# Routing beside attention in layer 0, and another order of work in layer 1, in a four-layer attention and expert stack

## The chip, the cores and the metric

The kernel runs on one core of one Trainium2 chip. The metric is the device time of one execution in microseconds (us). The core's engines are TensorE (PE; its weight loads are listed as PEld), VectorE (DVE), ScalarE (ACT), GpSimd (POOL) and SyncE (SP, which issues most transfers). Each has its own queue, taken in order, and they wait for each other through semaphores.

## The reference

`x` is 4 batches of 512 tokens of width 128, `ctx` 4 batches of 154 tokens. Eight residual steps follow each other: four layers, each an attention from x to ctx and then a mixture of 8 experts. What matters here:

```python
def _L0_xattn_ref(encoder_hc, decoder_hq, w_sim, b_sim, W_qv, b_qv):
    Sim = (encoder_hc @ w1)[:, :, None] + (decoder_hq @ w2)[:, None, :] + \
          jnp.einsum('bid,bjd->bij', encoder_hc * w3, decoder_hq) + b_sim[0]
    A = softmax(Sim, axis=2)
    hq_hat = jnp.einsum('bij,bjd->bid', A, decoder_hq)
    Batt = softmax(jnp.max(Sim, axis=2), axis=1)
    hc_bar = jnp.einsum('bi,bid->bd', Batt, encoder_hc)[:, None, :]
    hc_hat = jnp.broadcast_to(hc_bar, encoder_hc.shape)
    feats = concatenate([encoder_hc, hq_hat, encoder_hc * hq_hat, encoder_hc * hc_hat], axis=-1)
    return feats @ W_qv + b_qv

x = x + _L0_xattn_ref(_layernorm(x), ctx, ...)
x = x + _L0_ffn_ref(_layernorm(x), ...)           # top 2 of 8 experts, silu gate
x = x + _L1_xattn_ref(ctx, ctx, _layernorm(x), mask, ...)   # 16 heads of 8
x = x + _L1_ffn_ref(_layernorm(x), ...)           # top 1 of 8 experts, with a capacity
x = x + _L2_xattn_ref(...)                        # 16 heads of 64
...
```

Layer 1's attention is a masked softmax over the 154 context tokens for each of 16 heads of width 8, then the product with V and a projection by `Wo`.

## The kernel before, in words

Tokens are handled in tiles of 128: a batch has `NI` = 4 of them. Experts work on two halves, each of two batches. For a half, `route` computes norms, logits, the top experts, the rank of each token within its expert and from these a slot for each token (`su`) and a list of the expert of each block (`eb`). It is a generator: each `yield` is a point at which its caller can put other work, and `Steps.step(n)` advances it by n such steps. The normalised tokens are then written to their slots in DRAM by indirect transfers on POOL (`scatter`, L721). These row transfers are first put into a list, `rows_due`; `row_transfers(n, behind)` starts up to n of them, and with `behind` each of them waits for that instruction, so that they are paced by the work beside them. `experts` loads blocks of tokens (`tok`, L838, which waits for all row transfers of the half), transposes them (L848), multiplies them by the weights of their expert (`up`, L875; `down`, L906) and stores the results; `gather` puts indirect loads of the results (L939) into `rows_due`, and `combine` adds them to x (L957).

Layer 0's attention (`layer0_setup`) works on a whole batch at a time: `prepare(b)` normalises and transposes x, computes `Sim` as two products, one with the scaled context (L979) and one with the row term `w2b` (L980), copies it to SBUF with the scalar `bsim` added (L983, into `sim`, of which there is one buffer), and takes its maxima and exponentials. `tile_of` normalises the probabilities (L1004), transposes them (L1008, L1013), multiplies by the context, computes the batch-wide softmax (L1034 and L1036 are its weighted sum and its sum of weights), builds the last three of the four features (L1042 to L1044) and multiplies the four by W_qv (L1049). `attend_first` runs the four batches; the first half's routing is begun after batch 2's turn, and its row transfers come after all four batches. In this part the order of instructions on each engine is chosen by a planner, which takes the order of the program as priority and its own estimates of durations.

Layer 1's attention works tile by tile, in 16 periods, in an order written out by hand on PE, ACT and DVE (`attend_all`, `narrow_period`). A period holds the scores and exponentials of tile `new` beside the products with V of tile `old`. Scores come in three groups of heads: `score(g)` on PE (L1141 mask, L1150), `most(g)` on DVE (L291, the negated maximum), `exp(g)` on ACT (L305). `score(0)` and `most(0)` of the next tile, `nxt`, come at the end of a period. For `old`: `turn_ends` and `turn(n)` transpose the probabilities on PE, `take_ends` and `take(n)` copy them on DVE (L261), `by_v_ends` and `by_v(n)` are the products with V (L381, L405), and `scaled` multiplies by the inverse sums (L412). The inverse sums are spread over the partitions by `replicate`: a transposition (L332), a copy (`rT`, L334), a store to DRAM (L339) and a load (L340, `rep`). `project` (L422) and `residual` end a tile. `parts` prepares the next batch, one part in each of four periods: mask, norm and values, the transposed norm, keys and queries. `middle` and `after` take one step of the work beside: combining the experts' results of layer 0, then routing for layer 1.

PSUM holds two buffers of each of three kinds, given out in turn: `sc` for scores, `tr` for transposes and small products, `av` for products with V. A new use waits for the readers of the use before the last.

Of the kernel before, what the change touches and what calls it, by code (L numbers as in the profile page):

```python
# [19 lines left out]
P = 128  # L20
# [6 lines left out]
E = 8  # L27
# [19 lines left out]
def tile_xattn_moe_stack(ctx: ExitStack, tc: tile.TileContext, a: dict, out: bass.AP):  # L47
# [33 lines left out]
    turn = [0]  # L81

    def evac(o, i, scale=None):

        turn[0] += 1
        if turn[0] % 2:
            if scale is None:
                nc.vector.tensor_copy(o, i)
            else:
                nc.vector.tensor_scalar(o, i, scale, None, ALU.mult)  # L90
        elif scale is None:
            nc.scalar.copy(o, i)
        else:
            nc.scalar.activation(o, i, AF.Copy, scale=scale)
# [10 lines left out]
    x = []  # L105
    for b in range(B):
        t = xpool.tile([P, NI, D], F32, tag=f"x{b}", name=f"x{b}")
        nc.sync.dma_start(t, x_in[b])
        x.append(t)
# [3 lines left out]
    nc.sync.dma_start(ctail, a["ctx_1024"][:, P:S2, :].rearrange("b k d -> k b d"))  # L113

# [89 lines left out]
    def columns(src, rows, name):  # L204

        t = p2.tile([rows, P], F32, tag="rows", name=f"{name}_r")
        nc.sync.dma_start(t, src)
# [224 lines left out]
    def narrow_period(new, old, nxt=None, middle=nothing, queries=nothing, parts=nothing, after=nothing):  # L432
# [9 lines left out]
        if old:  # L442
            old.turn_ends()
            old.turn(0)
        if new:
            new.most(1)
            new.exp(0)
            new.exp(1)
        if old:
            old.take_ends("v")  # L450
            old.take(0, "v")
            old.by_v_ends()
            old.turn(1)
            old.take(1, "v")
        if new:
            new.score(2)
        if old:
            old.turn(2)
            old.by_v(0)
            old.by_v(1)  # L460
        if new:
            new.most(2)
            new.exp(2)
        if old:
            old.take(2, "v")
            old.turn(3)
            old.by_v(2)
            old.take(3, "v")
# [3 lines left out]
        parts()  # L472
        if nxt:
            nxt.score(0)
            nxt.most(0)
# [4 lines left out]
        if new:  # L480
            new.replicate()
        if old:
            old.project()
            old.residual()
        after()

    def wide_period(new, old, nxt=None, middle=nothing, queries=nothing, parts=nothing, after=nothing):
# [472 lines left out]
    def layer0_setup():  # L960
        wsim = columns(a["L0_xattn_w_sim"].rearrange("(k p) -> k p", p=P), 3, "wsim")
# [437 lines left out]
```

## Time and profile before

| | us |
|---|---|
| median of 3 runs | 1300.3 |
| lowest and highest | 1290.47, 1302.03 |
| profiled execution, its own time | 1392.88 |
| span of its instructions | 1390.8 |
| mean granted TensorE clock in it | 0.902 |

The profiled execution takes longer than the timed runs, so stages and sums are read in its own time and related to the median afterwards. In the groups of the page a line of a helper stands for all its callers: L261 is every copy by `copy` on DVE, L305 every exponential of layers 1 to 3. "[... <- X]" after a line of the timeline is the idle time of that engine before it and what ended it. "x2" counts instructions; an fp32 product is two of them.

### The profile page before, as it was taken

The page shows a single profiled execution, that of the slowest core. Times are in us where ns is not written, and L with a number is a line of the kernel's source. Part 1 is how long each engine was busy: PE and PEld are TensorE (multiplying, and loading weights), DVE is VectorE, ACT ScalarE, POOL GpSimd, SP SyncE. Part 2 cuts the span into 40 slices and gives each one's busy share as a digit, 9 for nine tenths or more (in the row PEclk, how much of TensorE's full clock was granted, in tenths as well). Part 3 has the DMA queues.
Part 4 walks back from the last instruction along what each step waited for, and adds up shares of the span by engine and source line. Part 5 has one row for each costly group of instructions (what it writes and reads, how often), then busy time and mean ns, then how long its engine had stood idle before and what let it go on. Part 6 is the DMA issues. An engine that isn't in the chain of part 4 may idle for free.

```text
span 1390.8 us, 26946 instructions
## 1 busy us (share of the span) xinstructions
PE 1125.7 (81%) x9435; PEld 924.2 (66%) x9435; DVE 736.2 (53%) x2057; ACT 575.6 (41%) x2290; POOL 252.9 (18%) x281
## 2 busy tenths in 40 slices
PE   5876998976777689788999988657879999898881
PEld 3766997833344348776878767646668778787771
DVE  4563546546667655235667665314456667454442
ACT  1113333543454444355665554212545655432220
POOL 2031314031000101302000031332220000304224
PEclk8787999968998879999999999767999999899996
DMA  6014685611010215532212224442321112245652
GB/s 210 1 65 118 207 251 182 196 51 29 9 22 27 70 27 141 148 98 47 47 32 56 54 66 121 120 124 80 116 47 39 40 33 47 66 109 142 179 163 69
DMA packets 136995, 126.80 MB, mean 91 GB/s; under 512 B 13466, under 2 KB 116511, under 8 KB 136479
## 3 DMA queue, kind: packets, MB, share of 16 engines
q1 hardware_dynamic: 129695, 110.39, 28.6%
q0 software_dynamic: 7168, 14.69, 3.7%
q8 instruction: 77, 1.26, 0.4%
q14 instruction: 55, 0.45, 0.1%
HBM read 101.31 MB, written 23.72 MB: 90 GB/s over the span
## 4 chain that ended last, share of the span: by engine, by line
PE 36%; DVE 8%; issue 4%; ACT 4%; DMA 4%; another core or an unknown queue 3%; POOL 1%; SPq 1%; POOLq 0%; DVEq 0%; ACTq 0%
PE sc L875 5%; PE sc L608 5%; PE av L405 4%; PE av L906 4%; PE tr L368 4%; PE tr L422 4%; DMA w<-in_up 3%; ACT probs L305 2%; PE sc L593 2%; PE av L387 2%; DVE nm L291 2%; PE sc L557 1%; POOL yg L939 1%; DVE aT L412 1%
## 5 line engine op out<-in xcount | busy, mean ns | idle before, releaser
L305 ACT ACTIVATE probs<-sc,nm 128x154 f32<-128x154 f32 x768 | 287.0, 402 | 193.6 <-DVE nm L291 178.4
L875 PE MATMUL sc<-tokT,w 128*128 128x128 f32 x1528 | 214.6, 290 | 19.8 <-DMA w<-in_up 14.8
L875 PEld LDWEIGHTS sc<-tokT,w 128*128 128x128 f32 x1528 | 195.0, 202 | 31.0 <-DMA w<-in_up 11.1
L906 PE MATMUL av<-w,hT 128*128 x1160 | 179.2, 292 | 42.7 <-issue 19.2
L291 DVE TENSOR_REDUCE nm<-sc 128x6 f32<-128x924 f32 x144 | 143.2, 1010 | 100.7 <-PE sc L608 47.9
L906 PEld LDWEIGHTS av<-w,hT 128*128 128x128 f32 x1160 | 155.9, 201 | 53.9 <-issue 22.9
L305 ACT ACTIVATION_READ_ACCUMULATOR probs<-sc,nm 128x1 f32 x768 | 168.0, 219 | 0.0
L939 POOL DMA_INDIRECT yg<-ybuf,su x112 | 107.0, 956 | 295.5 <-DVE ys L914 67.1
L233 POOL TENSOR_TENSOR rstd<-ve,nhalf 128x4 f32<-128x4 f32 x32 | 33.1, 1034 | 652.4 <-DVE ve L231 544.4
L721 POOL DMA_INDIRECT buf<-xn,su x112 | 108.4, 968 | 184.0 <-DVE eb L744 78.7
L261 DVE COPY pT<-tr 128x512 f32<-128x512 f32 x160 | 107.3, 687 | 62.0 <-PE tr L368 48.6
L368 PE MATMUL tr<-ident,probs 128*128 128x128 f32 x768 | 123.9, 293 | 0.7 <-DVE rT L334 0.7
L405 PE MATMUL av<-pT,vm 128*64 128x128 f32 (+1 forms) x1536 | 104.5, 285 | 18.4 <-DVE pT L261 16.8
L368 PEld LDWEIGHTS tr<-ident,probs 128*128 128x128 f32 x768 | 88.0, 148 | 29.4 <-issue 14.5
L914 DVE COPY ys<-av 128x128 f32<-128x128 f32 x168 | 48.0, 286 | 111.2 <-PE av L906 73.4
L405 PEld LDWEIGHTS av<-pT,vm 128*64 128x64 f32 (+1 forms) x1536 | 65.2, 127 | 46.8 <-DVE pT L261 25.9
L891 ACT ACTIVATE eg<-sc,w 128x128 f32<-128x128 f32 x184 | 52.9, 370 | 89.2 <-PE sc L875 52.2
L608 PE MATMUL sc<-kT,qT 64*128 64x154 f32 x1024 | 85.1, 304 | 3.5 <-ACT probs L305 3.5
L895 DVE SCALAR_TENSOR_TENSOR hT<-sc,w,eg 128x128 f32<-128x128 f32 x184 | 55.9, 342 | 53.4 <-ACT eg L891 50.6
L608 PEld LDWEIGHTS sc<-kT,qT 64*128 64x128 f32 x1024 | 69.8, 186 | 14.5 <-issue 10.1
L593 PE MATMUL sc<-xnT,wq 128*128 128x128 f32 x512 | 70.8, 296 | 2.9 <-ACT probs L305 2.9
L593 PEld LDWEIGHTS sc<-xnT,wq 128*128 128x128 f32 x512 | 64.9, 206 | 8.2 <-issue 4.3
(252 smaller groups left out, 1504.8 us busy)
## 6 DMA issues: line engine op xcount, KB each, us to landing
w<-in_up SPq DMA_DIRECT2D x46, 516.0 KB
w<-in_up SPq DMA_DIRECT2D x76, 258.0 KB
rep<-rd SPq DMA_DIRECT2D x64, 256.0 KB
ybuf<-ys SPq DMA_DIRECT2D x168, 64.0 KB
tok<-buf SPq DMA_DIRECT2D x36, 256.0 KB
w<-in_down SPq DMA_DIRECT2D x3, 2048.0 KB
w<-in_up SPq DMA_DIRECT2D x46, 128.0 KB
buf<-zero SPq DMA_DIRECT2D x2, 1472.0 KB
```

What stands on the lines that cost most here:

```text
L261: return nc.vector.tensor_copy(o, i)
L291: nc.vector.tensor_reduce(self.at.heads(self.nm, g, n), self.sc[g][:, :, 0 : n * S2].rearrange("p j (s k) -> p j s k", s=n), AX.X, ALU.max ...
L305: nc.scalar.activation(self.pr[:, h, :], self.sc[g][:, j, s * S2 : (s + 1) * S2], AF.Exp, bias=self.nm[:, h : h + 1], accum_out=self.rs[:, ...
L368: nc.tensor.transpose(q[:, t * P : (t + 1) * P], self.pr[:, h, 0:P], ident)
L405: nc.tensor.matmul(av[rows, cols], v, self.pT[n][:, t, :], start=False, stop=last)
L593: nc.tensor.matmul(sc[:, c // 4, c % 4 * P : (c % 4 + 1) * P], wq[:, c * P : (c + 1) * P], at.xnT[:, i * P : (i + 1) * P], start=True, sto ...
L608: nc.tensor.matmul(sc[:, j, s * S2 : (s + 1) * S2], at.qT[i][rows, c, :], at.kT[rows, c, :], start=True, stop=True)
L721: ins = nc.gpsimd.indirect_dma_start(out=buf[half], out_offset=bass.IndirectOffsetOnAxis(ap=su[:, t : t + 1], axis=0), in_=xns[t // NI][:, ...
L875: nc.tensor.matmul(dst, w[:, at : at + P], xT, start=True, stop=True)
L895: products.append(nc.vector.scalar_tensor_tensor(hT[:, fc, :], up, b0, g, ALU.add, ALU.mult))
L906: nc.tensor.matmul(y[:, 0:D], hT[:, fc, :], w2[:, bass.ds(e, 1), fc, :].rearrange("p o d -> p (o d)"), start=(fc == 0), stop=(fc == nf - 1),)
L939: ins = nc.gpsimd.indirect_dma_start(out=yg[:, t, :], out_offset=None, in_=ybuf[half], in_offset=bass.IndirectOffsetOnAxis(ap=su[:, t : t ...
```

## The change

In layer 0:
- `Sim`'s row term is computed once for all batches, with `bsim`, into `row`; `prepare` does one product a tile and adds `row` while copying. `sim` has two buffers.
- the product of x with the broadcast average is folded into the weights: `wc` is the first block of W_qv plus the fourth scaled by the average, and three products remain of four. The sum of weights is taken by the exponential's accumulator and one product.
- `attend_first` prepares a batch or two ahead, and begins routing after batch 1; row transfers go two at a time behind four instructions each of batches 2 and 3.
- the rows and the context are loaded ahead of the other inputs; the experts' gates are loaded after layer 0's own weights.

In layer 1:
- `nxt.score(0)` and `nxt.most(0)` come between `by_v(1)` and `turn(3)`; `parts` comes after `take(1)`; `middle` after the next maximum.
- `replicate` of `old` comes at the start of its period, after `score(1)`; `project` and `residual` come one period later (`older`).
- keys and queries use a `tr` and an `av` buffer instead of an `sc` buffer.
- `evac`, which alternates between DVE and ACT, uses DVE alone during this attention (`busy`).

`ordered_all` holds the same three engines that `ordered` held.

```diff
-        if turn[0] % 2:
+        if turn[0] % 2 or busy[0]:
...
-    def narrow_period(new, old, nxt=None, middle=nothing, queries=nothing, parts=nothing, after=nothing):
+    def narrow_period(new, old, nxt=None, middle=nothing, queries=nothing, parts=nothing, after=nothing, older=None):
...
         if new:
             new.score(1)
-        if old:
-            old.turn_ends()
-            old.turn(0)
-        if new:
             new.most(1)
             new.exp(0)
-            new.exp(1)
+        if older:
+            older.project()
+            older.residual()
         if old:
+            old.replicate()
+            old.turn_ends()
             old.take_ends("v")
+            old.turn(0)
             old.take(0, "v")
             old.by_v_ends()
             old.turn(1)
             old.take(1, "v")
+        parts()
         if new:
+            new.exp(1)
             new.score(2)
-        if old:
-            old.turn(2)
-            old.by_v(0)
-            old.by_v(1)
-        if new:
             new.most(2)
             new.exp(2)
         if old:
+            old.by_v(0)
+            old.turn(2)
             old.take(2, "v")
+            old.by_v(1)
+        if nxt:
+            nxt.score(0)
+            nxt.most(0)
+        if old:
             old.turn(3)
+            old.take(3, "v")
             old.by_v(2)
-            old.take(3, "v")
             old.by_v(3)
             old.scaled(0)
         middle()
-        parts()
-        if nxt:
-            nxt.score(0)
-            nxt.most(0)
         if new:
             new.short()
             new.inverse()
         queries()
-        if new:
-            new.replicate()
-        if old:
-            old.project()
-            old.residual()
         after()
...
+        row = w1.tile([P, B, S2], F32, tag="wv", name="row")
+        sc = ps_sc()
+        for j in range(2):
+            nc.tensor.matmul(
+                sc[:, j, 0 : 2 * S2],
+                w2b,
+                ctxT[:, 2 * j : 2 * j + 2, :].rearrange("p b k -> p (b k)"),
...
-                nc.tensor.matmul(dst, xnT[:, i * P : (i + 1) * P], rhs1[:, b, :], start=True, stop=False)
-                nc.tensor.matmul(dst, w2b, ctxT[:, b, :], start=False, stop=True)
-            sim = p2.tile([P, NI, S2], F32, tag="aT", name="sim", bufs=1)
+                nc.tensor.matmul(dst, xnT[:, i * P : (i + 1) * P], rhs1[:, b, :], start=True, stop=True)
+            sim = p2.tile([P, NI, S2], F32, tag="probs", name="sim")
...
-            evac(pm, q)
+            row_transfers(2, evac(pm, q))
...
-            evac(pt, q[0:ST, :])
+            row_transfers(2, evac(pt, q[0:ST, :]))
...
-            nc.scalar.activation(ebt, md, AF.Exp)
+            es = small.tile([P, 1], F32, tag="es", name="es")
+            nc.scalar.activation(ebt, md, AF.Exp, accum_out=es)
...
-            for i in range(NI):
-                nc.tensor.matmul(hcp[:, 1:2], ones, ebt[:, i : i + 1], start=(i == 0), stop=(i == NI - 1))
+            nc.tensor.matmul(hcp[:, 1:2], ones, es, start=True, stop=True)
...
+            wc = p2.tile([P, D], F32, tag="res1", name="wc")
+            nc.vector.scalar_tensor_tensor(wc, wqv[:, 3, :], hc, wqv[:, 0, :], ALU.mult, ALU.add)
+            ft = p2.tile([P, 2, S], F32, tag="vm", name="ft")
+            row_transfers(2, nc.scalar.copy(ft[:, 0, :], hq))
...
-                sc = ps_sc()
-                nc.tensor.matmul(sc[:, 0, 0:S2], bd["Wk"], ctxT[:, b, :], start=True, stop=True)
-                nc.tensor.matmul(sc[:, 1, :], bd["Wq"], at.xnT, start=True, stop=True)
+                k, q = ps_tr(), ps_av()
+                nc.tensor.matmul(k[:, 0:S2], bd["Wk"], ctxT[:, b, :], start=True, stop=True)
+                nc.tensor.matmul(q, bd["Wq"], at.xnT, start=True, stop=True)
...
-        beside = Steps(idle())
-        tiles = prepare(0, found[0])
-        for b in range(B):
-            tiles(0)
-            if b == 1:
-                found.update({k: stats(x[k]) for k in range(2, B)})
-            if b == 2:
-                beside = Steps(route(layer, 0, *gates[layer]))
-            if b < B - 1:
-                tiles = prepare(b + 1, found[b + 1])
-            if b == 2:
-                beside.step(6)
+        tiles = [prepare(b, found[b]) for b in range(2)]
+        tiles[0](0)
+        tiles.append(prepare(2, found[2]))
+        tiles[1](0)
+        beside = Steps(route(layer, 0, *gates[layer])).step(3)
+        tiles.append(prepare(3, found[3]))
+        beside.step(5)
+        tiles[2](0)
+        beside.step(1)
+        tiles[3](0)
         return beside.finish()
...
-        if last:
-            (narrow_period if layer == 1 else wide_period)(None, last)
+        if layer == 1:
+            narrow_period(None, last, older=late)
+            last.project()
+            last.residual()
+        elif last:
+            wide_period(None, last)
```

## The prediction

> **What bounds the kernel now.** I read the page first, then windows of busy time by stage, then the timeline where a window showed idle engines.
>
> ```profile
> span 1390.8 us, 26946 instructions
> PE 1125.7 (81%) x9435; PEld 924.2 (66%) x9435; DVE 736.2 (53%) x2057; ACT 575.6 (41%) x2290; POOL 252.9 (18%) x281
> PE   5876998976777689788999988657879999898881
> PEclk8787999968998879999999999767999999899996
> ```
>
> TensorE is the busiest engine, but over the span that average mixes stages. The change touches two: layer 0's attention (slices 1 to 4) and layer 1's attention (slices 8 to 15, where PE falls to 6 and 7 and the granted clock sags). The windows of layer 0, cut where each batch's scores are copied out and where the first expert product starts:
>
> ```profile
> core 0: us, PE busy (x) PEld busy (x) DVE busy (x) ACT busy (x) POOL busy (x), PEclk, DMA share, GB/s
> 36.66:53.88 17.22, 14.84 (x85) 12.53 (x84) 10.60 (x35) 3.10 (x11) 1.01 (x1) 0.80 0.00 1
> 53.88:70.85 16.97, 15.28 (x89) 12.97 (x88) 10.54 (x35) 3.70 (x12) 1.01 (x1) 0.80 0.00 1
> 70.85:93.91 23.06, 21.64 (x157) 19.37 (x156) 17.19 (x73) 4.34 (x14) 3.17 (x3) 0.85 0.04 9
> 93.91:117.59 23.68, 3.62 (x21) 2.74 (x20) 5.50 (x24) 0.00 (x0) 14.47 (x15) 0.58 0.37 128
> ```
>
> A batch takes 17 us, 85% of it PE work; then come 23.7 us in which PE works 3.6. The timeline says what fills them:
>
> ```profile
> 90.87 0.16 DVE L744 TENSOR_SCALAR eb<-ef 1x23 int32<-1x23 f32 x1
> 91.18 1.19 POOL L721 DMA_INDIRECT buf<-xn,su  x1 [8.46 <-DVE eb L744]
> ...
> 110.38 0.96 POOL L721 DMA_INDIRECT buf<-xn,su  x1 [0.30 <-issue]
> 112.77 5.28 SPq L838 DMA_DIRECT2D tok<-buf  x4
> 115.72 1.94 PE L848 MATMUL tr<-ident,tok 128*128 128x128 f32 x8 [15.59 <-DMA tok<-buf]
> 117.59 5.70 PE L875 MATMUL sc<-tokT,w 128*128 128x128 f32 x32
> ```
>
> The routing table is ready at 90.9; 16 row transfers of 1.26 us each follow one another on POOL until 111.3 (20.2 us); only then can the token load start, and PE waits for it.
>
> Layer 1 has 16 periods, cut here at the first maximum of each tile:
>
> ```profile
> 281.00:301.61 20.61, 13.24 (x83) 6.50 (x83) 8.78 (x18) 6.81 (x33) 7.65 (x8) 0.67 0.12 32
> 367.33:379.38 12.05, 9.35 (x85) 5.05 (x85) 8.15 (x16) 6.81 (x33) 0.00 (x0) 1.00 0.06 12
> 379.38:394.01 14.63, 10.15 (x85) 5.22 (x85) 8.91 (x15) 7.29 (x34) 0.00 (x0) 1.00 0.05 10
> 407.42:422.09 14.67, 9.40 (x85) 5.10 (x85) 11.65 (x37) 6.81 (x33) 2.02 (x2) 0.99 0.15 46
> ```
>
> No engine is full in any of them. A period is a chain of PE and DVE waiting for each other, 12 us at the least and 15.5 on average (272.35 to 520). The longest hold indirect transfers:
>
> ```profile
> 285.51 0.32 SPq L340 DMA_DIRECT2D rep<-rd  x1
> 299.58 0.29 DVE L412 TENSOR_TENSOR aT<-av,rep 128x128 f32<-128x128 f32 x1 [5.02 <-PE sc L1150]
> 371.75 0.32 SPq L340 DMA_DIRECT2D rep<-rd  x1
> 377.45 0.29 DVE L412 TENSOR_TENSOR aT<-av,rep 128x128 f32<-128x128 f32 x1 [0.55 <-PE av L405]
> ```
>
> The scaling that needs the replicated sums waited until 14 us after their load was issued in a period with eight row gathers; in a quiet one it was free 5.7 us after the issue.
>
> **What the skill says.** *DMA: Bandwidth & Descriptors*, section *Anatomy of one DMA*, gives a fixed cost of about 2 us a transfer; here L340, which waits for L339's data, follows it by 2.4 us (369.36 to 371.75), which agrees. *TensorE: Matmul & The Clock Gate*, section *Why this matters for your kernels*, says to leave no PE gap over some 3 us between bursts, or the clock falls to half; the trace agrees: 0.67 around the stalls of 281 to 301, 1.00 in 367 to 394. *DMA*, section *Queues, rings and completion order*: each DMA engine goes round its queue rows packet by packet; whether gathers hold up the load of the sums in this way, no run here shows.
>
> **The change, layer 0.** (a) PE work. The row product (L980) leaves every batch: 8 instructions at 0.13 us (0.26 at half clock), 1.0 to 2.1 us. The products with W_qv go from 32 to 24 at 0.11 to 0.21: 0.9 to 1.7. The sums with ones (L1036) go from 8 to 2 at 0.12: 0.7. Together 2.6 to 4.5, middle 3.4 at this clock; for four batches 13.6 less, and 4 instructions of twice the width come back once (1 to 2). (b) DVE: the 0.55 us product L1044 goes, a 128x128 one (0.35, L957's form) and a column one (0.15) come. The score copy takes a tensor operand instead of a scalar: L983 takes 0.53, the SBUF-only L1004 takes 0.80 for twice the width, so -0.1 to +0.1 each: nothing. ACT gains one 0.19 us accumulator read. (c) The routing starts after batch 1 instead of beside batch 3. PE work from 19.1 to 93.9 was 63.6 us of 74.8 (the windows shown and 11.8 in 19.1 to 36.7); it falls to 52. At the same busy share attention would end at 80 instead of 93.9; but its order is the planner's, and the routing's small DVE steps now stand among the copies, so I take half: 87. (d) The table: batch 1 was done at 64.9 and should be at about 56; from there the table took 26 us amid other work, and its own steps sum to some 14 (statistics and norm 4.5, transposes to logits 3.8, two maxima 2.4, ranks and slots 3), so it is ready between 70 and 82; the transfers then need 20.2, to 90 to 102. (e) Pacing holds the last pair behind the last batch's output copy, at about 86, to 89. POOL's other work is the 1 us powers of the norms: those of batches 2 and 3 stand behind the paced transfers, as they stood behind all 16 before (111.37). I take 93 for the last transfer against 111.3: **-18 us**, bounds -9 to -23. Loading rows and context ahead of the other inputs shortens the front by 1 to 2 us, which the wider row product takes back. What follows has PE busy 32 to 34 us of each 35 from 140 to 280, so the shift is kept.
>
> **Layer 1.** Take the plain order at full clock with the durations of 367 to 379: a score group 1.5 (the short one 1.1), four transposes 0.58, a copy 0.60 (0.69 to its end), a maximum 1.04, a product group 0.36, DVE to PE 0.2. Before: 12.05, or 11.5 without the 0.5 of xnT. After, from the start of score 1 at 0: score 1 to 1.5; projection and replication on PE to 2.0; maximum 1 to 2.6, residual's first step to 2.95. The projection and the end transposes use the same of two buffers, so these *now wait for the residual*: 3.15 to 3.75, turn 0 to 4.3, copies to 5.0, turn 1 to 5.55, score 2 to 6.65, by_v 0, turn 2, by_v 1 to 7.9, next score 0 to 9.4, turn 3 to 9.95, next maximum on DVE to 10.5, copy 3 to 11.1, last product 11.3 to 11.7. That is 11.7: the next scores do not wait any more, but 1.2 us are lost at the front and 1.0 before the last product. Plain periods: 0. Gains come where something stood between the last product and the next scores: three periods with values (norm, two products: DVE 2.0) and three with keys and queries (PE 1.5, DVE 1.43, ACT 0.6, in series). These now stand mid-period, yet cost PE and DVE time there, and the query copy delays exp 1: about 1 us each, 6 in all. Routing and combining steps (DVE 1.3 to 2.7) come after the next maximum: 0.4 in eight periods, 3. Against it: the mask of batches 2 and 3 shares buffers with the value ends, so its load starts after by_v_ends (344.65 before); now its use follows 1.2 us later instead of 4.7. Landing takes 2 to 4.7, so the DVE queue, with copies and maximum 2 behind it, waits 1 to 3.5 us twice; I take 1.5 each. Sum -6; the copies that DVE takes over from ACT lie in its slack of a third of a period. Last tile: one projection and one residual move into layer 1's experts, under 1 us. **-6 us**, bounds -20 (the stalls beside transfers shrink too) to +10 (lower clock by the new front wait).
>
> **Sum.** 1392.9 (the profiled execution; its span is 1390.8) - 24 = 1369. The median run is 1300.3, or 0.9335 of that; with it the saving is 22 us: **1278**. From here 1% is what a measurement can tell from no change: 1287.3 and 1313.3.
>
> **Rivals.** *Layer 0 gains, layer 1 loses what it gains* (front wait and mask wait weigh more; for: the hand count gives nothing in plain periods): -18 + 4 = -14, 1287. *Layer 1's transfer stalls go as well* (the first maximum now precedes them; for: some 20 us of periods 20.6, 19.1 and 23.7 are stall; against: no reason of theirs is removed): -24 - 15, 1264. *The routing isn't moved in effect*: the planner keeps the table behind attention, the 20 us stay, and only fewer products count: -10 in all, 1291. *Slower: the sums arrive late.* From the copy of the sums to the scaling it was 8.1 us in a quiet period (369.3 to 377.45); now it is 3.4 to 11.7, 8.3. If the load takes longer than 8.3, each period grows by the rest; if it takes the 12 to 14 us seen beside gathers everywhere, 15 periods grow by about 3.7: +55 - 18 = +37, 1335. It decides from about 11 us on. Against: the quiet periods bound it to 8.1.
>
> **How the numbers follow.** Forecast 0.44; layer 1 nothing 0.20; stalls go 0.14; routing not moved 0.11; sums late 0.11. The second is split at its edge (1287). Faster by over 1%: 0.44 + 0.14 + 0.10 = 0.68; within 1%: 0.10 + 0.11 = 0.21; slower 0.11. The range goes down past the rival at 1264 with the full -23 in layer 0, to 1258, and up to 1302, past the unmoved routing with layer 1 at +10.
>
> **What would show it.** Right: last row transfer of layer 0 near 93 and first expert product near 99; PE busy in that gap; layer 1 about 6 us shorter with a 1 us wait of the end transposes for the residual. Wrong: a table after 85, transfers still in a bare row, scalings that wait for a DMA in quiet periods, or a mean clock in layer 1 under 0.8.

## The result and the profile after

| | us |
|---|---|
| before, median of 20 runs | 1298.6 |
| after, median of 20 runs | 1291.2 (1281.5 to 1299.0) |
| ratio after / before | 0.9944, 95% interval 0.9924 to 0.9963 |
| forecast | 1278 (1258 to 1302) |

By the ratio the change saves 7.3 us, 0.56% (by its interval 4.8 to 9.9 us). The direction was as forecast, the size a third of the 22 us.

First the base. The profile that the forecast was worked on has a span of 1390.8 us; the kernel before, profiled again as `e0`, has one of 1299.7. One row of the groups, first from the forecast's profile and then from the new one (after the bars: busy time and mean of one, then the idle time ahead of the group and what ended it), shows what the first had besides:

```profile
L914 DVE COPY ys<-av 128x128 f32<-128x128 f32 x168 | 48.0, 286 | 111.2 <-PE av L906 73.4 <-remote 29.7 <-DMA w<-in_up 3.5
```

```profile
L914 DVE COPY ys<-av 128x128 f32<-128x128 f32 x168 | 48.2, 287 | 75.0 <-PE av L906 69.4 <-DMA ybuf<-ys 5.3
```

Same copies, same duration, but 29.7 us of idle time whose releaser the profile does not know ("remote"). Such stalls, up to 8.9 us long, stand in several groups of the forecast's profile; neither `e0` nor the profile after shows one. So the profiles below are read against `e0`. The page after, the span and three rows:

```profile
span 1289.8 us, 26803 instructions
PE 1094.4 (85%) x9351; PEld 897.6 (70%) x9351; DVE 739.7 (57%) x2066; ACT 572.4 (44%) x2290; POOL 252.4 (20%) x281
PE   4787998987877789889999989957899999899881
PEclk8668999998998789999999999879999999999996
```

The second and third digits of the clock row already show the surprise of layer 0: 6 and 6, where `e0` has 7 and 8 and an attention with less work was expected to be denser. Its windows, cut at the forecast's times (busy time and count of PE, PEld, DVE, ACT, POOL, then clock and DMA):

```profile
core 0: us, PE busy (x) PEld busy (x) DVE busy (x) ACT busy (x) POOL busy (x), PEclk, DMA share, GB/s
36.70:54.00 17.30, 14.30 (x75) 12.34 (x75) 10.26 (x36) 3.27 (x13) 1.01 (x1) 0.70 0.00 1
54.00:71.00 17.00, 8.55 (x37) 7.86 (x36) 10.11 (x42) 2.53 (x10) 1.01 (x1) 0.60 0.00 0
71.00:94.00 23.00, 21.28 (x108) 14.67 (x109) 13.22 (x57) 3.49 (x9) 13.69 (x14) 0.72 0.34 112
```

From 54 to 71, where the routing now stands, PE works 8.6 of 17 us instead of 15.3. The timeline of the way to the first expert product:

```profile
74.84 0.16 DVE L742 TENSOR_SCALAR eb<-ef 1x23 int32<-1x23 f32 x1
75.15 1.19 POOL L719 DMA_INDIRECT buf<-xn,su  x1 [16.29 <-DVE eb L742]
...
91.84 0.96 POOL L719 DMA_INDIRECT buf<-xn,su  x1 [0.30 <-issue]
...
99.12 0.69 DVE L1067 TENSOR_TENSOR x<-x,res 128x512 f32<-128x512 f32 x1
...
99.38 1.34 POOL L719 DMA_INDIRECT buf<-xn,su  x1 [4.30 <-DVE res L1065]
101.02 0.95 POOL L719 DMA_INDIRECT buf<-xn,su  x1 [0.30 <-issue]
...
103.41 0.95 SPq L836 DMA_DIRECT2D tok<-buf  x2
...
106.39 1.98 PE L846 MATMUL tr<-ident,tok 128*128 128x128 f32 x8 [6.58 <-DMA tok<-buf]
...
108.28 2.08 PE L873 MATMUL sc<-tokT,w 128*128 128x128 f32 x8
```

The table is ready at 74.8 (before 90.9), as forecast between 70 and 82. But attention ends at 99.8 (L1067) instead of 93.9 (94.3 in `e0`), and so the last pair of row transfers, held behind batch 3's output copy, starts 6.6 us after the pair before it has gone (92.8). The first expert product comes at 108.3: 9.3 earlier than before, where 18 were forecast.

Layer 1 is cut into 15 windows between the second maxima of neighbouring tiles. Two of them, before (`e0`) and after:

```profile
348.40:360.46 12.06, 9.35 (x86) 5.05 (x87) 8.17 (x14) 6.80 (x35) 0.00 (x0) 1.00 0.07 13
449.84:466.57 16.73, 12.42 (x98) 7.16 (x99) 10.14 (x20) 7.48 (x36) 7.77 (x8) 0.90 0.36 109
```

```profile
335.83:347.66 11.83, 9.65 (x86) 4.91 (x87) 8.04 (x14) 6.80 (x33) 0.00 (x0) 1.00 0.07 13
439.74:460.29 20.55, 17.25 (x103) 9.97 (x103) 11.82 (x26) 7.94 (x41) 8.78 (x9) 0.68 0.33 97
```

The plain period shown is the same to 0.2 us, as forecast. The period with routing products is 3.8 us longer. Two more windows grew, the fifth by 1.7 us and the ninth by 2.9: in each of them VectorE now waits about 3 us for the mask. Below, "layer 1's stage" is the time from the first maximum of layer 1 to the first of layer 2: 309.3 before (`e0`), 311.9 after.

### The profile page after: what moved, and what is told of

Read it like the earlier page. It is cut to its first block, busy times and chain, and to the rows that moved or that the text cites. A ratio compares the mean times of both kernels' runs of the same rounds, so it can differ in the third digit from the quotient of the medians.

```text
span 1289.8 us, 26803 instructions
## 1 busy us (share of the span) xinstructions
PE 1094.4 (85%) x9351; PEld 897.6 (70%) x9351; DVE 739.7 (57%) x2066; ACT 572.4 (44%) x2290; POOL 252.4 (20%) x281
## 4 chain that ended last, share of the span: by engine, by line
PE 61%; DVE 14%; DMA 10%; issue 6%; ACT 5%; POOL 2%; SPq 2%; POOLq 0%; DVEq 0%; ACTq 0%
PE sc L873 11%; PE tr L370 7%; PE av L904 6%; PE av L407 6%; PE sc L606 5%; DMA w<-in_up 5%; PE tr L424 5%; DVE nm L293 3%; PE sc L1159 3%; PE sc L591 3%; ACT probs L307 3%; PE av L389 2%; PE tr L357 2%; DMA yg<-ybuf,su 2%; PE tr L846 2%
## 5 line engine op out<-in xcount | busy, mean ns | idle before, releaser
L873 PE MATMUL sc<-tokT,w 128*128 128x128 f32 x1528 | 211.3, 287 | 23.8 <-DMA w<-in_up 19.2
L873 PEld LDWEIGHTS sc<-tokT,w 128*128 128x128 f32 x1528 | 190.4, 198 | 37.0 <-DMA w<-in_up 14.0
L904 PE MATMUL av<-w,hT 128*128 x1160 | 168.3, 282 | 4.1 <-DVE hT L893 2.5
L904 PEld LDWEIGHTS av<-w,hT 128*128 128x128 f32 x1160 | 148.5, 195 | 11.1 <-DVE hT L893 3.7
L407 PE MATMUL av<-pT,vm 128*64 128x128 f32 (+1 forms) x1536 | 106.0, 285 | 17.2 <-DVE pT L263 17.1
L912 DVE COPY ys<-av 128x128 f32<-128x128 f32 x168 | 48.1, 286 | 74.2 <-PE av L904 67.2
L591 PE MATMUL sc<-xnT,wq 128*128 128x128 f32 x512 | 68.2, 289 | 2.9 <-ACT probs L307 2.9
```

What stands on the lines that cost most here:

```text
L407: nc.tensor.matmul(av[rows, cols], v, self.pT[n][:, t, :], start=False, stop=last)
L591: nc.tensor.matmul(sc[:, c // 4, c % 4 * P : (c % 4 + 1) * P], wq[:, c * P : (c + 1) * P], at.xnT[:, i * P : (i + 1) * P], start=True, sto ...
L873: nc.tensor.matmul(dst, w[:, at : at + P], xT, start=True, stop=True)
L904: nc.tensor.matmul(y[:, 0:D], hT[:, fc, :], w2[:, bass.ds(e, 1), fc, :].rearrange("p o d -> p (o d)"), start=(fc == 0), stop=(fc == nf - 1),)
```

## Experiments

Each line of the table gives the median beside that of the kernel before in the same comparison, the ratio with its interval, and, from the one profile of each, the time of the first expert product and layer 1's stage.

| kernel | us / before | ratio | first product | stage |
|---|---|---|---|---|
| e1 layer 0 alone | 1287.1 / 1298.7 | 0.9924 (0.9900, 0.9948) | 109.5 | 307.0 |
| e2 layer 1 alone | 1300.8 / 1298.7 | 1.0024 (1.0001, 1.0047) | 114.3 | 314.8 |
| e3 rows not held | 1287.4 / 1298.7 | 0.9923 (0.9901, 0.9945) | 105.2 | 313.7 |
| e4 projection later | 1276.6 / 1298.0 | 0.9845 (0.9804, 0.9885) | 104.2 | 304.8 |
| e5 routing as before | 1286.5 / 1298.0 | 0.9913 (0.9879, 0.9946) | 105.1 | 313.3 |
| e6 layer 0 alone, rows not held | 1281.7 / 1298.0 | 0.9897 (0.9855, 0.9939) | 103.6 | 307.8 |
| e7 e3 and e4 | 1278.2 / 1298.0 | 0.9848 (0.9814, 0.9882) | 102.6 | 304.1 |
| e8 e5 and e4 | 1280.7 / 1300.6 | 0.9861 (0.9826, 0.9895) | 104.0 | 304.3 |
| e9 routing between batches 2 and 3 | 1282.7 / 1300.6 | 0.9889 (0.9854, 0.9925) | 106.0 | 307.6 |
| e10 one batch ahead | 1290.7 / 1300.6 | 0.9930 (0.9909, 0.9951) | 107.9 | 315.8 |
| e11 replication later | 1283.1 / 1300.6 | 0.9881 (0.9843, 0.9919) | 105.0 | 309.0 |
| e12 idle products | 1387.5 / 1403.8 | 0.9883 (0.9852, 0.9914) | 110.0 | 333.6 |
| e13 e8, idle products | 1367.2 / 1403.8 | 0.9744 (0.9711, 0.9778) | 103.5 | 320.2 |
| e14 e4 again | 1369.4 / 1403.8 | 0.9774 (0.9737, 0.9812) | 108.8 | 312.8 |
| e15 changed kernel again | 1387.1 / 1403.8 | 0.9888 (0.9856, 0.9920) | 108.7 | 329.4 |
| e17 e7 again | 1280.9 / 1306.1 | 0.9826 (0.9793, 0.9859) | 103.5 | 303.7 |
| e18 e7, routing step ahead | 1262.6 / 1297.3 | 0.9728 (0.9692, 0.9765) | 104.6 | 293.2 |

**The base and the two halves.** `e0` is the kernel before, once more.

> The kernel before, unchanged, profiled once more. The profile that the forecast was worked on took 1392.9 us where timed runs take 1299, and some 100 us of its idle time was put down to another core or an unknown queue; the profile of the changed kernel has no such entry and takes 1289.8. Theory: those stalls belong to that one execution. Then this one takes 1290 to 1307, its layer 1 attention (first maximum of tile 0 to the last maximum) takes about 220 us instead of 244.6, and its first expert product of layer 0 stays near 117.6, since layer 0 showed no such stall. Rival: the stalls are the kernel's own and the changed kernel removes them; then they are here again and layer 1 takes about 240.

1301.7 us, layer 1's maxima 213.2 apart, first expert product at 117.9, no stall of the unknown kind: they belong to the execution, not to the kernel.

`e1` has layer 1 as before (old `narrow_period`, `keys_queries` and last period, `busy` off), `e2` has layer 0 as before.

```diff
-        busy[0] = layer == 1
+        busy[0] = False
...
-            narrow_period(None, last, older=late)
-            last.project()
-            last.residual()
+            narrow_period(None, last)
```

> Layer 0 as in the changed kernel, layer 1 as before. The changed kernel's first expert product comes at 108.3 instead of 117.6 (-9.3). Theory A, layer 0 carries it all and layer 1 gives a little back: 9 us less than before, about 1289.5, ratio 0.993. Theory B, as forecast in its proportions (three quarters to one): -5.5, about 1293. Theory C, layer 1 carries half of it or more: -4 or less, 1295 and above.

> Layer 1's attention as in the changed kernel, layer 0 as before. Theory A: no gain, 0 to +3 us, 1299 to 1302, because the end transposes wait for the residual (19.7 us in 14 periods of the changed kernel) where the old order waited for the inverse sums (32 us in 15 periods). Theory B: -2. Theory C: -4 or more, 1295 and below.

Theory A: by the ratios layer 0 gives 9.9 us (11.6 between the medians) and layer 1 takes 3.1 back (2.1 between the medians; by the interval 0.1 to 6.1). The sum, 6.8, is near the whole change's 7.3.

**Layer 0: the holds.** `e3` and `e6` start all transfers once the table is ready:

```diff
-            row_transfers(2, evac(pm, q))
+            evac(pm, q)
...
         beside.step(5)
+        row_transfers()
         tiles[2](0)
```

> The changed kernel with one thing taken away: the 16 row transfers of layer 0 wait for no instruction of batches 2 and 3; all are started as soon as the routing table is ready. In the changed kernel 14 of them ran one every 1.26 us from 75.15 to 92.8, and the last two waited until 99.38 for the output copy of batch 3. Theory: the hold of the last pair sets the end of the transfers; without it the last ends at 75.15 + 16 x 1.26 = 95.4 instead of 102, the first expert product moves from 108.3 to 102, and the time falls by 6.5 us, to about 1285. Rival: the experts can't start before attention's own end at 99.8, or the powers of the norms now stand behind the transfers on GpSimd and delay batch 3: then -2 us or nothing.

> Layer 0 as in the changed kernel with the row transfers held by nothing, layer 1 as before. If the two effects add up: layer 0 alone took 1287.1, and freeing the transfers took 3.8 us from the changed kernel, so 1283.3. If the holds only mattered together with the changed layer 1: 1287.

The last transfer ended at 95.2, as worked out, but the first product came only 3.1 us earlier: batch 3's output products kept PE until 98.2, and the combining bias (L798, 2.1 us from 99.9) and transposes of the second half stood ahead of the experts' products. By the ratios the times fall by 2.7 us and, with the old layer 1, by 3.5, but the intervals overlap, and `e7` beside `e4` shows no gain in time (1278.2 and 1276.6). The profiles tell it better, taken together: in the six with early routing and held transfers the first product comes at 104.2 to 110.0, on average 108.2; in the five with free transfers at 102.6 to 105.2, on average 103.9. The hold costs some 4 us at that point; behind it attention's own end is the next bound.

**Layer 0: the routing's place.**

```diff
         tiles[1](0)
-        beside = Steps(route(layer, 0, *gates[layer])).step(3)
-        tiles.append(prepare(3, found[3]))
-        beside.step(5)
         tiles[2](0)
-        beside.step(1)
+        beside = Steps(route(layer, 0, *gates[layer]))
+        tiles.append(prepare(3, found[3]))
+        beside.step(6)
         tiles[3](0)
```

> The changed kernel with layer 0's routing begun where it was before (after batch 2, beside batch 3), its row transfers after all four batches; products merged and row term alone as in the changed kernel. Theory: PE work removed from attention is handed back by a lower granted clock (66 TensorE instructions fewer between the first score copy and attention's end in the changed kernel, but 62.1 us busy against 63.2 before), so that the merged products bring 3 us at most: the table is ready near 89, the first expert product comes near 114 to 117 and the time is 1297 to 1301. Rival: with the routing out of the way attention keeps its clock and ends 8 us or more earlier, taking the table and the transfers along: first expert product at 110 or before, time 1292 or less, as in the changed kernel.

The rival won, and my first explanation (that the clock takes back what the merged products save) fell with it. The timeline of `e5`:

```profile
78.30 0.16 DVE L742 TENSOR_SCALAR eb<-ef 1x23 int32<-1x23 f32 x1
...
81.01 0.67 DVE L1067 TENSOR_TENSOR x<-x,res 128x512 f32<-128x512 f32 x1
...
97.99 0.96 POOL L719 DMA_INDIRECT buf<-xn,su  x1 [0.30 <-issue]
...
103.22 1.94 PE L846 MATMUL tr<-ident,tok 128*128 128x128 f32 x8 [15.87 <-DMA tok<-buf]
105.09 3.09 PE L873 MATMUL sc<-tokT,w 128*128 128x128 f32 x19
```

Without the early routing attention ends at 81.7, 12 us before the old 94, and takes the table along to 78.3. Begun early, the routing brings the table forward by only 3.5 us more and pushes attention's end back by 18. In the window 54 to 71 PE works 15.7 of 17 us at a clock of 0.90 here, 8.6 at 0.60 in the changed kernel: there the queue of PE, taken in order, stood 4.4 us for the routing's norm (L242) and 4.1 for its selection (L684), with batches 2 and 3 behind. The whole way from 19 us to attention's end, first in the changed kernel, then in `e5`:

```profile
19.00:99.81 80.81, 61.51 (x289) 48.58 (x288) 45.30 (x169) 14.83 (x53) 17.17 (x18) 0.66 0.23 77
```

```profile
19.00:81.68 62.68, 50.82 (x273) 41.09 (x274) 41.65 (x161) 14.89 (x54) 5.48 (x6) 0.75 0.20 65
```

Of the 18.1 us, PE stands idle for 7.4 and is busy for 10.7. Of the busy part 2.5 are bias products (L798) that now come before attention's end; most of the rest is the same work at a clock of 0.66 instead of 0.75. So the waits are not all of it: the clock that is lower with them has a share, and no run parts the two. Nor did the early start pay once its transfers were free: the four profiles with routing as before have their first product at 103.5 to 105.1, on average 104.4, half a microsecond from the 103.9 above.

`e10` is `e5` with `prepare(1)` and `prepare(2)` moved behind the batch before each.

> The version with routing begun as before, and batches prepared one ahead as in the kernel before, instead of two ahead; products merged, row term alone, inputs loaded in the new order. It parts the gain of layer 0 (first expert product 117.9 to 105.1, -12.8). If the removed products carry it (the forecast's 13.6 us over four batches): attention ends near 83 and the time is within 2 us of 1286.5. If preparing ahead carries it, because batch 0 then has other work in its gaps (batch 0 took 29 us from its score copy to its end before, 23 with two ahead): attention ends near 88 to 90 and the time is 1292 to 1295.

In between: attention ends at 84.3, first product 107.9. By these single profiles preparing two ahead brings 2.8 of the 12.8 us, and the rest (10) is merged products, row term and order of loads together; these three were not parted, and 2.8 us is less than two profiles of one order can differ by (below). `e9` is `e8` with the routing's first eight steps between batch 2 and `prepare(3)`:

> As the version with both edits, but layer 0's first eight routing steps stand behind batch 2 and ahead of the preparation of batch 3, instead of behind that preparation; the row transfers start as soon as the table is ready. Theory: the routing beside batch 2 cost attention its speed because it came ahead of batch 2's products; behind them it fills gaps: the table comes near 75 instead of 78.3, attention ends near 84 instead of 81.7 and, as the transfers set the end, the first expert product moves from 105.1 to about 102: 3 us less than the version with both edits. Rival: batch 3 now waits as batches 2 and 3 did in the changed kernel, attention ends after 95 and nothing is gained.

The rival: attention ended at 104.2, the table came no earlier (78.1). (Its layer 1 is that of `e8`, and yet its stage is 307.6 against 304.3.)

**Layer 1: the projection's place.** The waits of layer 1 in the changed kernel (total, times, longest):

```profile
PE tr L357 <- DVE res L1173: 19.7, 14, 3.1
DVE madd L1106 <- DMA mi<-in_mask_Bx1xSxS_if: 6.0, 2, 3.1
```

```diff
-        if older:
-            older.project()
-            older.residual()
         if old:
             old.replicate()
             old.turn_ends()
...
             old.by_v_ends()
+        if older:
+            older.project()
+            older.residual()
+        if old:
             old.turn(1)
```

> The changed kernel with the projection and the residual of the older tile moved in layer 1 from ahead of the end transposes to behind the end products, so that the end transposes wait for no residual. Theory: in the changed kernel TensorE idled 19.7 us in 14 periods at that place (up to 3 us at once) and its granted clock in layer 1 fell with it (0.79 to 0.89 in several periods where the kernel before had 0.91 to 1.00), so that the same products took 165 us instead of 151. Without the wait each period loses about 1.2 us of its chain and the clock rises again: layer 1's attention falls from 217.8 to 195 to 205, the time by 12 to 20 us, to 1272 to 1279. Rival: the wait only moves, to the first products with V or to the next scores, since the same work on VectorE precedes them: within 4 us of the changed kernel, 1287 to 1294.

> The changed kernel with both: row transfers of layer 0 held by nothing, and layer 1's projection behind the end products. If both effects add up: 3.8 us below the version with the projection alone moved, so 1268 to 1275. If the projection's move brings nothing: 1287.

> The changed kernel with two edits that each gained alone: layer 0's routing begun as before (1286.5 alone) and layer 1's projection behind the end products (1276.6 alone). If they add up, as they lie in different stages: the changed kernel's 1291.2 less 4.7 and 14.6, 1272. If one of them was a lucky draw: 1277 to 1283.

The wait for the residual is gone. With this order of layer 1 the stage is 303.7 to 307.6 in five profiles (`e4`, `e7`, `e8`, `e9`, `e17`), from 311.9 to 315.8 in the five with the changed order: 9.0 us between the means. The stage in `e0`, in the changed kernel and in `e4`:

```profile
268.82:578.08 309.26, 242.06 (x2009) 160.16 (x2010) 184.00 (x458) 156.07 (x672) 46.61 (x48) 0.95 0.26 70
```

```profile
258.83:570.70 311.87, 255.17 (x2009) 164.22 (x2010) 185.09 (x462) 153.24 (x668) 46.59 (x48) 0.92 0.25 70
```

```profile
255.89:560.65 304.76, 255.16 (x2009) 165.28 (x2010) 185.45 (x462) 153.47 (x668) 46.71 (x48) 0.92 0.26 71
```

From the changed kernel to `e4` PE is busy for the same time at the same clock, so these 7.1 us are idle time that went, and no gain of clock. So `e4` came out at the expected time (1276.6) and not by the expected way: from first to last maximum layer 1 took 209.2 us, not 195 to 205, and some 4 us more came from layer 0, which the edit does not touch. Much of the 7.1 lies in the two windows with the mask, which shrink by 2.6 and 3.5 us, while the plain window shown above loses 0.4. Between the start of the mask's load and its use VectorE now works 1.7 us instead of 0.7 and 0.0, and its two waits fall from 6.0 us to 2.4. The times don't add up as neatly as the stages: `e7` and `e8` should each be some 4 us below `e4` and are not; their intervals are 9 to 11 us wide. A first product at 104.2 in `e4` and 108.3 in the changed kernel, with the same order in layer 0, shows that one profile's draw is worth 4 us.

`e11` is `e8` with `replicate` moved behind the end products too, because in `e4` PE still waited nearly as long at the next place:

```profile
PE tr L370 <- DVE rT L336: 17.1, 15, 2.7
```

> As the version with both edits, and layer 1's replication of the inverse sums moved from ahead of the end transposes to behind the end products too. With the projection moved, TensorE still idled 17.1 us in 15 periods until the copy of the inverse sums freed the buffer of the first transposes, up to 2.7 us at once, and two periods ran at a granted clock of 0.68. Theory: this wait goes as the first did, and layer 1 falls by another 4 to 8 us, 1264 to 1268 if the version with both edits takes 1272. Rival: VectorE is behind at that place, so the same time is spent waiting for the copy of the end transposes, and the load of the sums comes 2 us later: no change to 3 us slower.

The rival: the wait moved to the copy of the end transposes (L383 for `tails`, 20.3 us), and the stage is 309.0 against 304.3. VectorE is late at that place.

**Layer 1: wait or clock?** In the changed kernel the clock falls after such a wait. Windows of 2 us behind the one at 438.2 (3.0 us):

```profile
440.00:442.00 2.00, 0.81 (x4) 0.83 (x5) 1.91 (x6) 2.00 (x13) 0.00 (x0) 0.60 0.93 259
442.00:444.00 2.00, 2.00 (x16) 1.29 (x15) 1.71 (x4) 1.22 (x8) 1.01 (x1) 0.50 0.54 163
444.00:446.00 2.00, 2.00 (x10) 1.13 (x8) 1.50 (x5) 0.00 (x0) 1.56 (x2) 0.50 0.11 35
...
448.00:450.00 2.00, 2.00 (x18) 0.83 (x10) 0.85 (x2) 1.60 (x7) 1.66 (x2) 1.00 0.20 66
```

Half speed from 440.4 to 447.2, some 6 us of it with PE busy again, then full. The Trainium skill's *TensorE: Matmul & The Clock Gate*, section *Part 1: The HAM clock gate*, describes these two states, with a return after at least one busy window of some 3.4 us, and the trace agrees: each stretch at half speed in this stage lasts 3.4 or 6.8 us. To tell whether this is the loss, `e12` fills the wait with products that nobody reads, `e13` does so in `e8`; `e14` (`e4` again) and `e15` (the changed kernel again) ran beside them.

```diff
             nc.tensor.transpose(q[0:H, 0:P], self.rinv, ident)
+            if self.nb == 1:
+                for k in range(6):
+                    nc.tensor.matmul(q[:, P : 2 * P], ident, ident, start=True, stop=True)
             rT = small.tile([H, P], F32, tag="rT", name="rT", bufs=2)
```

> The changed kernel with six more products a period in layer 1 that nobody reads (identity by identity, into free columns of the buffer of the replication's transposition), at the place where TensorE waits for the residual: 96 products, some 0.7 us a period at full clock, inside a wait of 1.4 us. Theory: layer 1 lost by its granted clock, which goes to 0.5 for some 4 us after each wait of 2 us or more (half-clock time in layer 1 some 48 us in the changed kernel, 24 in the kernel before); with the wait partly filled fewer of these drops come, the mean clock in layer 1 rises from 0.89 to 0.94 and layer 1's attention shrinks by 4 to 8 us although work was added: 1283 to 1287 where the changed kernel takes 1291. Rival: the wait itself, not the clock, is the loss: then the time stays within 2 us, or grows by up to 5 where the products are longer than the wait.

> The version with layer 0's routing as before and the projection behind the end products (1280.7 in its own comparison, layer 1 207.8), with four such products a period where TensorE waits for the copy of the inverse sums. Theory of the clock: two periods at 0.68 become normal, 3 to 6 us less, ratio to the kernel before near 0.982. Rival: no change, 0.986.

> The changed kernel with the projection behind the end products once more, on the same chip as the changed kernel itself. Its first comparison gave 0.9845 of the kernel before, 14.6 us below the changed kernel, while its layer 1 was 8.6 us shorter in the profiles and its layer 0, with the same order of instructions, 4 us shorter. Theory: 8 to 10 us are the edit's and the rest is the draw of the executions: 1281 to 1284. Rival: it is all the edit's: 1277.

In this comparison every execution, the kernel before too (1403.8), took some 7% longer, and the four profiles have the stalls of the forecast's profile, so the four stand only beside each other: changed kernel 1387.1, `e12` 1387.5, `e14` 1369.4, `e13` 1367.2. (`e8` did not run beside `e13`, so what the idle products do there can't be told.) Layer 1 from the first tile's second maximum to the last maximum, changed kernel (`e15`) and `e12`, and in `e12` the wait:

```profile
269.80:498.00 228.20, 172.86 (x1272) 87.79 (x1271) 146.54 (x331) 105.99 (x517) 28.11 (x29) 0.87 0.14 40
```

```profile
269.00:498.50 229.50, 184.36 (x1452) 105.77 (x1451) 147.00 (x331) 106.22 (x517) 28.28 (x29) 0.91 0.14 40
```

```profile
PE tr L360 <- DVE res L1176: 4.3, 3, 1.8
```

The clock rises from 0.87 to 0.91, the wait is filled, and the time stays. So the higher clock brought nothing, and the clock theory has no support here. It is not ruled out: the idle products of a period take 1.5 us at full clock (L337 at 354.3), longer than the mean wait (17.8 us in 14 in `e15`), and the stage is 4 us longer; so where the wait was short they may have cost what the clock gave. The reading that fits both `e12` and `e4` is that the chain behind the wait costs (maximum, two steps of the residual, end transposes, their copy), and with it the mask, whose two waits of over 3 us `e12` leaves as they were. Taking the residual out of the chain brings 17.7 us under these conditions (`e14`), 16.6 of them in the stage, so the gain of `e4` is more than a draw.

**Layer 1: the steps beside.** The PE timeline of the long period of the changed kernel:

```profile
452.51 1.03 PE L790 MATMUL tr<-ident,comb 128*8 128x128 f32 x8 [0.64 <-DVE comb L781]
453.88 3.65 PE L798 MATMUL av<-b,cT 8*128 8x128 f32 x16 [0.33 <-DVE cT L88]
457.45 0.95 PE L1150 MATMUL sc<-madd,ident_b 128*128 128x462 bf16 x2
458.33 1.91 PE L1159 MATMUL sc<-kz,qT 64*128 64x462 f32 x4
```

Two routing steps (transposes L790, then 16 bias products L798) run one behind the other after the last product with V, and the next tile's scores (L1150, L1159) wait for both. `e18` is `e7` with one of the two steps ahead of the next scores in batches 2 and 3:

```diff
             old.by_v(1)
+        ahead()
         if nxt:
             nxt.score(0)
...
-                    period(new, old, nxt, step, queries, parts, after, older)
+                    if layer == 1 and b >= 2:
+                        period(new, old, nxt, nothing, queries, parts, after, older, step)
+                    else:
+                        period(new, old, nxt, step, queries, parts, after, older)
```

> The version with free row transfers and the projection moved, and one more edit in layer 1: in batches 2 and 3 the first of a period's two routing steps stands ahead of the next tile's scores again, as in the kernel before, instead of behind the last product. In the changed order both steps come between the last product and the next score(1), so that their own products run in series with it: the period with the routing's bias products took 20.6 us against 16.7 before, the one with its logits 16.7 against 15.5. Theory: these two periods shrink by 3 to 4 us together, and layer 1's stage (first maximum of layer 1 to first maximum of layer 2) falls from 304.1 to about 300.5. Rival: VectorE's part of the step now stands ahead of the next maximum and delays it in each routing period, which eats it up: stage within 1 us of 304 or longer.

```profile
427.33 1.03 PE L794 MATMUL tr<-ident,comb 128*8 128x128 f32 x8 [0.65 <-DVE comb L785]
428.20 0.55 PE L1152 MATMUL sc<-madd,ident_b 128*128 128x462 bf16 x2
428.68 1.05 PE L1161 MATMUL sc<-kz,qT 64*128 64x462 f32 x4
430.20 0.66 PE L370 MATMUL tr<-ident,probs 128*128 128x128 f32 x4 [0.47 <-DVE cT L88]
```

Now the next scores run while VectorE copies `cT`. The stage falls to 293.2, from 303.7 for `e7` run again in another comparison (1280.9 beside 1306.1): -10.5 where 3 to 4 were expected. All four windows with routing products and steps gain, 2.9, 2.6, 1.0 and 4.4 us. The stage in `e7` again (`e17`) and in `e18`:

```profile
254.09:557.79 303.70, 251.74 (x2009) 161.71 (x2010) 185.13 (x462) 153.59 (x668) 46.73 (x48) 0.93 0.27 72
```

```profile
255.16:548.33 293.17, 246.09 (x2009) 158.25 (x2010) 184.91 (x462) 153.45 (x668) 46.61 (x48) 0.95 0.26 74
```

PE stands idle 4.9 us less, near what was expected, and as many instructions take 5.6 us less at a higher clock. Both came with the new order of the steps; how much the clock alone is worth was not tried. At 1262.6 (0.9728) this version beats both kernels.

## Why the prediction was wrong, by its own steps

- **(a), (b) the work removed in layer 0**: right in the main. With the routing out of the way attention ended at 81.7, 12 us early, where the full share of the sum gave 80; by `e10` some 10 us of it are the removed work with the new order of loads, and 2.6 come from preparing two batches ahead, which (a) did not count. VectorE's score copies cost less than before (0.86 a pair against 0.98).
- **(c) attention's end, 87**: the step that failed. I halved the gain because the routing's small steps stand among the copies; they cost not 7 us but 18. PE's queue is in order and waits for them: PE was idle 7.4 us more. It was also busy 10.7 us more, most of that at the lower clock, which this step left out. The end was 99.8, later than before.
- **(d) the table, 70 to 82**: right, 74.8. But most of that came from the shorter batches, not from the earlier start: 78.3 without it.
- **(e) the pacing**: the mechanism was right, the last pair behind batch 3's output copy; with (c) that copy came at 98.4 instead of 86. So -9 instead of -18, the lower bound of that step.
- **Layer 1, plain periods 0**: right (11.83 against 12.06). The wait of the end transposes for the residual was 1.4 us on average, 19.7 in 14 periods, where 1.2 were named.
- **Layer 1, the gains of 6 and 3**: the other step that failed. That the values, keys, queries and routing steps no longer stand ahead of the next scores was counted as a gain. A step behind the last product is ahead of the next score(1) on PE, and there it runs bare. By `e18` the place of one of the two routing steps alone is worth 10 us of stage, the higher clock with it; the parts of the next batch were not tried apart.
- **Layer 1, the mask**: mechanism right, size too small: 6.0 us over two waits instead of 3.0, and 4.6 us in the two windows; with the projection moved the waits are 2.4.
- **Layer 1's sum**: -6 forecast, +2 to +3 in time (+6 in the stage, 313.9 against 308.0, the means of five and three profiles). The new order did take idle time out: in the stage PE is idle 56.7 us instead of `e0`'s 67.2. But as many PE instructions (2009) take 255.2 us instead of 242.1, at a clock of 0.92 instead of 0.95. The forecast named a lower clock only in its bound; how much of the loss it makes stays open, as `e12` does not settle it. With the projection out of the front the stage is 304.9 on average, 3.1 under the old order, half of the forecast's 6.
- **Sum**: the profile with foreign stalls was scaled by 0.9335, which took only 2 us off the saving; it did mislead the reading of the 19 to 24 us periods. The nearest rival, that layer 1 loses what layer 0 gains (1287), had the right sign for layer 1; the one that gave 1291 (routing not moved in effect) had the number by chance, for the table did move.

## What to carry to other kernels

In a queue taken in order, a chain of small steps that goes back and forth between engines makes everything behind it wait. Put independent work between its steps, as `e18` does with the next scores, and not the whole chain ahead of that work, as in layer 0. Before moving a chain ahead of its rivals, ask what the transfers it feeds will wait for: here the table came 3.5 us earlier, and attention, whose end held the last transfers, ended 18 us later. And profile the kernel before a second time when its profile is 7% off its timed runs.

## What was not expected of the hardware

Executions near 1400 us occur for the same kernel that mostly takes 1299, and in one comparison all of them were such: in their profiles VectorE and ScalarE stand still for up to 10 us at a time with no releaser (in `e15` 34.3 us in 7 times ahead of L882's activations). What does this stays open. The change is worth more there, 16.7 us (0.9888, interval 0.9856 to 0.9920). And a wait of 2.2 us on TensorE (291.3 in the changed kernel) was enough for a granted clock of 0.50 afterwards, where the Trainium skill's *TensorE: Matmul & The Clock Gate*, section *Why this matters for your kernels*, warns of gaps over some 3 us. The forecast's own profile, which it took as agreeing with that, shows the same: the half clock that starts there at 295.6 follows a wait of 2.6 us (292.0), and the longer one, of 4.8 us, comes only at 298.2.
